# Masked attention on one core: column sums of the exponentials taken by ScalarE's accumulator

## The chip, the cores and the metric

The kernel runs on one core of one Trainium2 chip. The metric is the device time of one execution, in microseconds (us). Before the change, three runs took 752.6, 754.56 and 755.21 us; the median is 754.56.

## What is computed

A residual masked self-attention of 8 batches, 512 features, 1024 tokens, 8 heads of 64 features; queries, keys and values are the same projection. `cond_2048` is the 0/1 mask `mask` of shape (8, 1024).

```python
xt = jnp.transpose(x, (0, 2, 1))
q = xt @ Wq.T
qh = q.reshape(B, T, NH, dk).transpose(0, 2, 1, 3)
scores = scale * jnp.einsum('bhqd,bhkd->bhqk', qh, qh)
logits = (scores * cmask + (1.0 - cmask) * NEG) * rmask
attn = jax.nn.softmax(logits, axis=-1)
ctx = jnp.einsum('bhqk,bhkd->bhqd', attn, qh)
out = ctx.transpose(0, 2, 1, 3).reshape(B, T, D) @ Wo.T
return x + jnp.transpose(out, (0, 2, 1))
```

A kept token attends to the kept tokens. A masked token's logits are all zero, so it gets the mean over all tokens.

## The kernel before

About half the tokens of a batch are kept. The kernel counts them, and where every batch has fewer than 544 it works on 544 columns (`NK`): the kept tokens, packed by an indirect DMA, columns that belong to no token, and as the last column the mean of x, for the masked tokens. Two halves of `KH` = 272 columns make a row of queries. Scores are symmetric, so the sum over the queries in a key's row of the transposed score block is that token's softmax denominator.

The 512 features are four **pairs** of heads, so the program runs over 32 pairs: four per batch, called pair 0 to pair 3 below (`pr` in the code). For each pair there are five **slots** (`k` = 0 to 4): first the short last key block (`LAST`, 32 keys and their copies, tile `el`), then the four key blocks of 128 (tiles `e`). The order of all engines is written out by hand in `late`: each slot issues the scores and exponentials of its block and then whatever the tables and `slots_of` put there.

- `scores` (L605, L609): score matmuls into PSUM tiles `s` (a ring of two tiles of two banks), then exponentials on ScalarE into `e`. Its bias is the tile `bias`.
- `add_up` (L626): sums over the valid queries on VectorE, as a product with a 0/1 row `valid` and an accumulator, one per head and block.
- `invert` with `inverses` (L704 to L709), in slot 0 of the next pair: the sums' inverses, which go to DRAM and come back as rows `rb`; `contexts` in slot 4 multiplies with them.
- `attend_short`, `attend_half` (L642): the products `av` of a pair, in slots 0, 1 and 2 of the next pair.
- `project` (L529) in slot 3 makes `qT` of the pair after next; `values` (L551, L554) in slot 4 transposes it to `v`. `lengths_of` (L563, L565, L572) in slot 1 squares `v` and reduces to `top`; `bias_of` (L578 on TensorE, L580 to L583 on VectorE) in slot 3 (slot 4 in one pair) turns `top` and makes the next pair's `bias`.

Work on other batches lies between. In pairs 0 and 1, `turn` (L417) transposes the next batch's x on VectorE in slots 2 and 4 of pair 0 and 0 and 1 of pair 1, into a ring of two tiles `xt`, and SP stores each to DRAM (`xd`, L425). `search` (L473) finds in pair 1 which token goes to which column, and `gather` (L485) on GpSimd fetches them. `add_features` (L436) sums features on ScalarE with an accumulator in pairs 0 and 1. `output` (L760) multiplies the previous batch's contexts in slots 3 and 4 of pair 1. `finish_blocks` (L829, L832), two operations a step, adds the residual on VectorE from slot 4 of pair 2 to slot 1 of pair 0, eight steps; after the last one SP stores the batch (L839).

SP's DMA queue is in order. Stores wait in the list `stores`, which `issue_stores` empties at the end of a slot, a batch's store one slot later than it was made:

```python
def issue_stores():
    for store in stores[1]:
        store()
    stores[1] = stores[0]
    stores[0] = []
```

Of the kernel before, what the change touches and what calls it, by code (L numbers as in the profile page):

```python
# [305 lines left out]
def attention_of_kept_tokens(ctx, tc, x, mask, wq, wo, out, ident, wqT, woT, verdict, flag):  # L306
# [34 lines left out]
    count = keep.tile([P, LONG], F32, name="count")  # L341
    quadrant = keep.tile([P, A], F32, name="quadrant")
# [10 lines left out]
    sums = [keep.tile([P, 2, NC], F32, name=f"sums_{i}") for i in range(2)]  # L353
# [10 lines left out]
    xs, xbars, xmeans, xds, xins, xcs, valids, searches = {}, {}, {}, {}, {}, {}, {}, {}  # L364
# [13 lines left out]
    def queries_of(b):  # L378

        valid = sb.tile([P, NK], F32, tag="valid", name=f"valid_{b}")  # L380
        nc.gpsimd.tensor_scalar(valid, count[:, :NK], kept[:, b : b + 1], None, ALU.is_lt)  # L381
        part = sb.tile([P, KH], F32, tag="part", name=f"part_{b}")
        for r in range(2):
            rows = slice(r * DK, (r + 1) * DK)
            nc.gpsimd.tensor_copy(part[rows, :], valid[rows, r * KH : (r + 1) * KH])
        valids[b] = valid, part

    def turn_first(i):
# [5 lines left out]
        if i == 0:  # L394
            xds[0] = dr.tile([T, D], F32, tag="xd_0", name="xd_0", bufs=1)
# [13 lines left out]
    def turn(b, i):  # L409
# [4 lines left out]
        if i == 0:  # L414
            xds[b] = dr.tile([T, D], F32, tag="xd", name=f"xd_{b}")
# [50 lines left out]
    def search(b, i):  # L466
# [10 lines left out]
            source[:, col], found[:, col], float(i * P), float(T - 1), ALU.add, ALU.min  # L477
# [42 lines left out]
    def project(pair, hf):  # L520
        b, pr = pair
        nm = f"{b}_{pr}"
        if hf == 0:
            qTs[pair] = sb.tile([P, W], F32, tag="qT", name=f"qT_{nm}", bufs=4)
# [11 lines left out]
        nc.scalar.copy(qT[:, cols], pq[:, :KH])  # L536
# [49 lines left out]
    es, rbs, cTs = {}, {}, {}  # L586

    def scores(pair, c):
        qT, nm = qTs[pair], "%d_%d_%d" % (*pair, c)
        heads = [slice(h * DK, (h + 1) * DK) for h in range(2)]  # L590
        keys = slice(c * P, c * P + (P if c < LAST else DK))
        if c < LAST:
# [4 lines left out]
        for hf in range(2):  # L597
            queries = slice(hf * KH, (hf + 1) * KH)
            to = slice(0, P)
            if c < LAST:  # L600
                s = ps.tile([P, 2, NB], F32, tag="s", name=f"s_{nm}_{hf}")
            else:
                to = slice(hf * DK, (hf + 1) * DK)
            for h in range(2):
                nc.tensor.matmul(  # L605
                    s[to, h, :KH], qT[heads[h], keys], qT[heads[h], queries], start=True, stop=True
                )
            if c < LAST or hf == 1:
                nc.scalar.activation(  # L609
                    e[:, hf if c < LAST else 0, :, :],  # L610
                    s[:, :, :KH],
                    AF.Exp,
                    bias=biases[pair][:, c : c + 1],
                    scale=SCALE,
                )
# [687 lines left out]
```

## Time and profile before

| | |
|---|---|
| median of three runs | 754.56 us (752.6 to 755.21) |
| the profiled execution | 753.0 us, of which the span on the core is 751.3 |
| busy, TensorE matmuls | 658.5 us |
| busy, VectorE | 532.7 us |
| busy, ScalarE | 375.8 us |
| busy, GpSimd | 173.2 us |
| mean granted TensorE clock | 0.925 |

The span is what the profile shows from the first to the last instruction. Busy time is the time in which at least one instruction of the engine ran; matmuls overlap, so their mean durations don't add up to it. PE is TensorE, PEld its weight loads, DVE VectorE, ACT ScalarE, POOL GpSimd, SP and SPq the queue that issues most DMAs. The granted clock is 1.00 at 2.4 GHz and 0.50 at 1.2 GHz. In a row of a timeline, brackets give how long the engine stood idle before it and whose result ended that.

### The profile page before, as it was taken

To read this page: it belongs to the slowest core of one execution; us is meant where nothing else is said; L and a number is where in the kernel's file an instruction comes from. 1 tells how busy PE (TensorE), PEld (TensorE's weight loads), DVE (VectorE), ACT (ScalarE), POOL (GpSimd) and SP (SyncE) were. 2 spreads that over 40 slices of the span, in tenths; PEclk is the share of its full clock that TensorE was granted. 3 is DMA by queue.
4 is the path that set the end of the run, shared out by engine and by line. 5 is a ranking of instruction groups with operands and counts; after the bars stand their busy time and mean duration, and the time that the engine had idled before them with its cause. 6 is when DMAs were issued, how large, how long until landed. Compare 5 with 4: busy or idle time off the path is not lost.

```text
span 751.3 us, 12016 instructions
## 1 busy us (share of the span) xinstructions
PE 658.5 (88%) x4139; PEld 399.7 (53%) x4139; DVE 532.7 (71%) x1560; ACT 375.8 (50%) x771; POOL 173.2 (23%) x222
## 2 busy tenths in 40 slices
PE   5789996999789998799789997799977998999962
PEld 4656664565454655456455664456544565655432
DVE  6179979449992698738996399835999269736761
ACT  5477675266443664256662564526643465425300
POOL 4712010350113410143102511035011440015030
PEclk9799998999889998899988998899988999999985
DMA  7544145845586347934488454774468530654247
GB/s 283 174 138 132 50 149 132 208 135 176 130 196 184 113 159 186 206 126 130 163 201 211 132 158 142 195 186 143 163 154 192 165 114 18 175 139 135 57 137 212
DMA packets 96703, 116.41 MB, mean 155 GB/s; under 512 B 10304, under 2 KB 74304, under 8 KB 96624
## 3 DMA queue, kind: packets, MB, share of 16 engines
q1 hardware_dynamic: 79552, 74.07, 37.4%
q0 software_dynamic: 12848, 39.30, 15.9%
q10 hardware_dynamic: 4224, 2.10, 1.0%
q8 instruction: 36, 0.59, 0.3%
q14 instruction: 43, 0.35, 0.2%
HBM read 72.78 MB, written 42.65 MB: 154 GB/s over the span
## 4 chain that ended last, share of the span: by engine, by line
PE 49%; DVE 37%; DMA 5%; issue 5%; ACT 2%; SPq 1%; POOL 1%; DVEq 0%; POOLq 0%
PE po L760 14%; DVE junk L626 10%; PE pq L529 10%; PE s L605 8%; PE av L642 7%; DVE xt L417 4%; DVE junk L473 4%; DVE o L829 3%; DVE xr L832 3%; PE xc L498 3%; DVE len L565 2%; DVE cT L744 2%; DMA xd<-xt 2%; PE pa L780 2%; DVE rb L739 2%
## 5 line engine op out<-in xcount | busy, mean ns | idle before, releaser
L626 DVE CUSTOM_DVE_ANT_0 junk<-e,valid 128x544 f32<-128x544 f32 x256 | 184.7, 721 | 54.1 <-ACT e L609 47.0
L609 ACT ACTIVATE e<-s,bias 128x544 f32<-128x544 f32 x256 | 168.9, 711 | 29.4 <-PE s L605 25.2
L605 PE MATMUL s<-qT 64*128 64x272 f32 (+1 forms) x1280 | 175.9, 418 | 1.3 <-ACT e L609 1.0
L529 PE MATMUL pq<-xc,wqT 128*128 128x272 f32 x512 | 153.0, 462 | 0.0
L529 PEld LDWEIGHTS pq<-xc,wqT 128*128 128x128 f32 x512 | 117.3, 235 | 28.2 <-issue 0.8
L642 PE MATMUL av<-e,v 128*64 128x272 f32 x1024 | 131.4, 399 | 0.0
L605 PEld LDWEIGHTS s<-qT 64*128 64x128 f32 (+1 forms) x1280 | 92.0, 174 | 71.0 <-issue 30.7
L760 PE MATMUL po<-woT,cT 128*128 128x512 f32 (+1 forms) x448 | 105.5, 434 | 0.0
L536 ACT COPY qT<-pq 128x272 f32<-128x272 f32 x64 | 24.6, 385 | 152.4 <-PE pq L529 152.4
L642 PEld LDWEIGHTS av<-e,v 128*64 128x64 f32 x1024 | 67.9, 136 | 56.0 <-issue 23.1
L485 POOL DMA_INDIRECT xin<-xd,source x40 | 41.5, 1038 | 212.4 <-DVE sums L626 88.0
L760 PEld LDWEIGHTS po<-woT,cT 128*128 128x128 f32 (+1 forms) x448 | 47.7, 150 | 52.7 <-issue 50.7
L861 POOL DMA_INDIRECT g<-od,block_origin x56 | 58.4, 1043 | 33.6 <-issue 17.1
L578 PE MATMUL top<-ident,top 128*128 128x128 f32 x32 | 12.1, 379 | 58.0 <-DVE top L572 57.8
L626 DVE CUSTOM_DVE_ANT_0 junk<-el,part 128x272 f32<-128x272 f32 x64 | 28.3, 442 | 45.9 <-ACT el L609 43.8
L769 POOL DMA_DIRECT2D od<-oc x56 | 30.1, 541 | 130.7 <-ACT oc L767 126.9
L767 ACT COPY oc<-po 128x512 f32<-128x512 f32 (+1 forms) x35 | 18.3, 522 | 81.8 <-PE po L760 81.8
L381 POOL TENSOR_SCALAR valid<-count,kept 128x544 f32<-128x544 f32 x8 | 13.1, 1642 | 138.6 <-DVE sums L704 138.5
L565 DVE TENSOR_REDUCE len<-sq 128x10 f32<-128x640 f32 x32 | 26.0, 813 | 25.7 <-ACT sq L563 25.6
L665 ACT COPY cT<-av 128x272 f32<-128x272 f32 x62 | 23.9, 385 | 39.1 <-PE av L642 39.1
L578 PEld LDWEIGHTS top<-ident,top 128*128 128x128 f32 x32 | 4.8, 151 | 70.9 <-DVE top L572 66.8
L473 DVE TENSOR_SCALAR_CACHE_REDUCE junk<-rank,key 128x1024 f32<-128x1024 f32 (+4 forms) x40 | 39.8, 996 | 1.9 <-ACT rank L1039 1.4
(139 smaller groups left out, 700.7 us busy)
## 6 DMA issues: line engine op xcount, KB each, us to landing
x<-in_x_dram SPq DMA_DIRECT2D x56, 256.0 KB
xd<-xt SPq DMA_DIRECT2D x112, 128.0 KB
xr<-in_x_dram SPq DMA_DIRECT2D x28, 512.0 KB
out_dram<-xr SPq DMA_DIRECT2D x24, 512.0 KB
rb<-row SPq DMA_DIRECT2D x60, 160.0 KB
od<-oc POOLq DMA_DIRECT2D x28, 256.0 KB, 2.5
rank<-ranks SPq DMA_DIRECT2D x6, 512.0 KB
xd<-xt POOLq DMA_DIRECT2D x8, 256.0 KB, 4.5
```

The source lines that it names most:

```text
L417: nc.vector.transpose(xt.rearrange("p k (d f) -> p k d f", d=ND), xs[b][r][:, :, at : at + n].rearrange("p d (k t) -> p k d t", t=Q),)
L473: nc.vector.tensor_scalar(junk[:, :n], rank[:, i * P :], key[:, col], 0.0, ALU.is_le, ALU.add, accum_out=found[:, col])
L485: nc.gpsimd.indirect_dma_start(out=xin[:n, :], out_offset=None, in_=xds[b], in_offset=bass.IndirectOffsetOnAxis(ap=searches[b][2][:n, i : ...
L529: nc.tensor.matmul(pq[:, :KH], wqT[:, d, pr * P : (pr + 1) * P], xcs[b][:, d, cols], start=(d == 0), stop=(d == ND - 1),)
L565: nc.vector.tensor_reduce(lengths, sq.rearrange("p c (h d) -> p (c h) d", h=2), axis=AX.X, op=ALU.add,)
L605: nc.tensor.matmul(s[to, h, :KH], qT[heads[h], keys], qT[heads[h], queries], start=True, stop=True)
L609: nc.scalar.activation(e[:, hf if c < LAST else 0, :, :], s[:, :, :KH], AF.Exp, bias=biases[pair][:, c : c + 1], scale=SCALE,)
L626: nc.vector.tensor_tensor_reduce(junk[:, :n].rearrange("p (f k) -> p f k", k=KH), e[:, :, h, :], (valid if c < LAST else part).rearrange(" ...
L642: nc.tensor.matmul(av[head, :KH], v[keys, c, head], e[keys, hf if c < LAST else 0, h, :], start=(c == first), stop=(c == last),)
L760: nc.tensor.matmul(po[k * n : (k + 1) * n, :w], cTs[b, pr][:, i * P : i * P + n], woT[:, pr, k * w : (k + 1) * w], start=(pr == 0), stop=( ...
L769: nc.gpsimd.dma_start(ods[b][places[i], k * w : (k + 1) * w], oc[k * n : (k + 1) * n, :w])
L861: nc.gpsimd.indirect_dma_start(out=g, out_offset=None, in_=ods[b], in_offset=bass.IndirectOffsetOnAxis(ap=block_origin[:, b, i : i + 1], a ...
```

## The change

The sums over the queries move from VectorE to ScalarE, whose accumulator adds up what an exponential writes. An exponential now covers one head and both halves of the queries, where it covered both heads and one half; so a block's two PSUM tiles hold one head each. The accumulator can't skip columns: those that belong to no token are made zero (the gather takes them from a row of zeros at the end of `xd`, and the mean's column of `qT` stays zero, its value is kept in the copies at the row's end). Each such column adds exp(bias) to a sum; `share` is that exponential, `lacks` the negative count of those columns, and `inverses` takes the product away. The short block `el` is still summed on VectorE (`add_ends`). The values' copy out of PSUM moves from slot 4 to slot 0 of the next pair, behind `el`.

```diff
+    rings = [keep.tile([P, W], F32, name=f"qT_{i}") for i in range(4)]
+    lacks = keep.tile([P, B], F32, name="lacks")
...
-            xds[b] = dr.tile([T, D], F32, tag="xd", name=f"xd_{b}")
+            xds[b] = dr.tile([T + 1, D], F32, tag="xd", name=f"xd_{b}")
+            nc.sync.dma_start(xds[b][T : T + 1, :], zero)
...
-            source[:, col], found[:, col], float(i * P), float(T - 1), ALU.add, ALU.min
+            source[:, col], found[:, col], float(i * P), float(T), ALU.add, ALU.min
...
-        nc.scalar.copy(qT[:, cols], pq[:, :KH])
+        n = KH - hf
+        nc.scalar.copy(qT[:, hf * KH : hf * KH + n], pq[:, :n])
...
     def scores(pair, c):
...
         if c < LAST:
             e = sb.tile([P, 2, 2, KH], F32, tag="e", name=f"e_{nm}", bufs=6)
+            ss = [ps.tile([P, 2, NB], F32, tag="s", name=f"s_{nm}_{h}") for h in range(2)]
+            for hf in range(2):
+                for h in range(2):
+                    nc.tensor.matmul(
+                        ss[h][:, hf, :KH],
+                        qT[heads[h], keys],
+                        qT[heads[h], queries[hf]],
+                        start=True,
+                        stop=True,
+                    )
+            for h in range(2):
+                nc.scalar.activation(
+                    e[:, :, h, :],
+                    ss[h][:, :, :KH],
+                    AF.Exp,
+                    bias=bias,
+                    scale=SCALE,
+                    accum_out=sums[pair[1] % 2][:, h, c : c + 1],
+                )
...
+            share = sb.tile([P, LAST], F32, tag="share", name=f"share_{nm}")
+            nc.scalar.activation(share, biases[pair][:, :LAST], AF.Exp)
...
-    def add_up(pair, c):
+    def add_ends(pair):
 
         b, pr = pair
-        valid, part = valids[b]
-        e = es[pair, c]
+        e = es[pair, LAST]
         for h in range(2):
...
             nc.vector.tensor_tensor_reduce(
-                junk[:, :n].rearrange("p (f k) -> p f k", k=KH),
-                e[:, :, h, :],
-                (valid if c < LAST else part).rearrange("p (f k) -> p f k", k=KH),
-                1.0,
-                0.0,
-                ALU.mult,
-                ALU.add,
-                sums[pr % 2][:, h, c : c + 1],
+                junk[:, :KH], e[:, 0, h, :], parts[b], 1.0, 0.0, ALU.mult, ALU.add, ends[pr % 2][:, h : h + 1]
             )
...
-        for h in range(2):
-            nc.vector.tensor_tensor(acc[:, h, :], acc[:, h, :], pads[:, b, :], ALU.add)
-        nc.vector.tensor_tensor(low, low, acc[:, :, :LAST], ALU.min)
-        nc.vector.tensor_scalar(acc[:, :, :LAST], acc[:, :, :LAST], TINY, None, ALU.max)
+        full = shares.pop(pair)
+        nc.vector.scalar_tensor_tensor(
+            full, full, lacks[:, b : b + 1], pads[:, b, :LAST], ALU.mult, ALU.add
+        )
+        nc.vector.tensor_tensor(acc, acc, full.unsqueeze(1).to_broadcast([P, 2, LAST]), ALU.add)
+        nc.vector.tensor_tensor(low, low, acc, ALU.min)
+        nc.vector.tensor_scalar(acc, acc, TINY, None, ALU.max)
...
-            todo[4].append(lambda: values(ahead))
+            todo[4].append(lambda: turn_values(ahead))
...
-                if k:
-                    add_up(pair, order[k - 1])
+                if k == 0 and p + 1 < len(pairs) and pairs[p + 1] in turned:
+                    copy_values(pairs[p + 1])
+                if k == 1:
+                    add_ends(pair)
                 if k == 0 and before:
-                    add_up(before, order[-1])
```

How the instructions lie afterwards, at three places. First VectorE, from the end of a batch's pair 3 into pair 0 of the next batch (`o` and `xr` are a finish step, `rt` the turned inverses). Before:

```order
L745 COPY cT_2_3491<-qT_2_2940 128x1
L829 STREAM_TRANSPOSE o_5_3612<-g_5_3484 128x512
L832 TENSOR_TENSOR xr_3092<-o_5_3612,xr_3092 128x16x32
L626 ISA junk_3_3_0_3632,sums_87<-e_3_3_3593,valid_2038 128x544
L626 ISA junk_3_3_1_3634,sums_87<-e_3_3_3593,valid_2038 128x544
L704 TENSOR_TENSOR sums_87<-sums_87,pads 128x5 x2
L705 TENSOR_TENSOR low<-low,sums_87 128x8
L706 TENSOR_SCALAR sums_87<-sums_87 128x2x4
L708 RECIPROCAL ris_89<-sums_87 128x2x4
L709 COPY ris_89<-sums_87 128x2
L718 STREAM_TRANSPOSE rt_3_3642<-ris_89 128x32
L829 STREAM_TRANSPOSE o_6_3652<-g_6_3509 128x512
```

The same place with the change:

```order
L772 COPY cT_2_1757<-qT_93 128x1
L856 STREAM_TRANSPOSE o_5_1865<-g_5_1750 128x512
L859 TENSOR_TENSOR xr_1384<-o_5_1865,xr_1384 128x16x32
L728 SCALAR_TENSOR_TENSOR share_3_4_1715<-share_3_4_1715,lacks,pads 128x4
L731 TENSOR_TENSOR sums_88<-sums_88,share_3_4_1715 128x8
L732 TENSOR_TENSOR low<-low,sums_88 128x8
L733 TENSOR_SCALAR sums_88<-sums_88 128x8
L735 RECIPROCAL ris_97<-sums_88 128x2x4
L736 TENSOR_SCALAR ris_97<-ends_90,pads 128x2
L745 STREAM_TRANSPOSE rt_3_1893<-ris_97 128x32
L856 STREAM_TRANSPOSE o_6_1903<-g_6_1775 128x512
```

The two sums over `e` are gone, and the inverses follow the finish step directly; all other places with a 128x544 sum lose it in the same way.

Second ScalarE, at the change from pair 0 to pair 1. Before:

```order
L609 ACTIVATE e_0_3_2134<-s_0_3_0_2135,bias_0_1930 128x544
L609 ACTIVATE e_0_3_2134<-s_0_3_1_2139,bias_0_1930 128x544
L554 COPY v_2_2155<-v_2_0_2156 128x512
L554 COPY v_2_2155<-v_2_4_2162 128x128
L609 ACTIVATE el_1_4_2169<-s_1_4_2170,bias_1_2110 128x544
L609 ACTIVATE e_1_0_2215<-s_1_0_0_2216,bias_1_2110 128x544
```

With the change:

```order
L628 ACTIVATE e_0_3_2015,sums_87<-s_0_3_0_2016,bias_0_1832 128x2x272
L628 ACTIVATE e_0_3_2015,sums_87<-s_0_3_1_2017,bias_0_1832 128x2x272
L645 ACTIVATE el_1_4_2043<-s_1_4_2044,bias_1_1996 128x544
L647 ACTIVATE share_1_4_2050<-bias_1_1996 128x4
L571 COPY v_2_2052<-v_2_0_2032 128x512
L571 COPY v_2_2052<-v_2_4_2037 128x128
L628 ACTIVATE e_1_0_2090,sums_88<-s_1_0_0_2091,bias_1_1996 128x2x272
```

The exponentials write `sums` too, `share` is new, and the copies of `v` stand behind `el`.

Third TensorE, the score matmuls at the same change of pairs. Before:

```order
L605 MATMUL s_1_4_2170<-qT_1_1939 64x272 x4
L642 MATMUL av_0_0_2204<-el_0_4_1985,v_0_1793 64x272 x2
L642 MATMUL av_0_1_2205<-el_0_4_1985,v_0_1793 64x272 x2
L605 MATMUL s_1_0_0_2216<-qT_1_1939 128x272 x2
L605 MATMUL s_1_0_1_2220<-qT_1_1939 128x272 x2
```

With the change:

```order
L642 MATMUL s_1_4_2044<-qT_92 64x272 x4
L666 MATMUL av_0_0_2079<-el_0_4_1875,v_0_1717 64x272 x2
L666 MATMUL av_0_1_2080<-el_0_4_1875,v_0_1717 64x272 x2
L620 MATMUL s_1_0_0_2091<-qT_92 128x272
L620 MATMUL s_1_0_1_2092<-qT_92 128x272
L620 MATMUL s_1_0_0_2091<-qT_92 128x272
L620 MATMUL s_1_0_1_2092<-qT_92 128x272
```

The matmuls are the same four, but they go to the two tiles by turns, where they filled one and then the other.

## Rows read from the trace of the kernel before

**Rows 1.** The page's first section: busy us, share of the span, instructions.

```profile
PE 658.5 (88%) x4139; PEld 399.7 (53%) x4139; DVE 532.7 (71%) x1560; ACT 375.8 (50%) x771; POOL 173.2 (23%) x222
```

**Rows 2.** TensorE's waits: us in total, times, longest us.

```profile
PE top L578 <- DVE top L572: 57.8, 21, 5.7
```

**Rows 3.** Windows: us, busy PE, PEld, DVE, ACT, POOL; clock, DMA share, GB/s.

```profile
101.56:115.76 14.20, 14.20 (x110) 8.85 (x102) 13.43 (x43) 11.20 (x26) 2.56 (x3) 1.00 0.24 63
169.61:184.29 14.68, 14.25 (x110) 8.84 (x102) 14.13 (x39) 8.83 (x18) 0.00 (x0) 1.00 0.47 159
184.29:206.04 21.75, 17.06 (x110) 10.72 (x102) 20.71 (x56) 11.33 (x26) 2.45 (x3) 0.84 0.54 146
241.36:258.12 16.76, 16.76 (x138) 11.03 (x130) 8.99 (x28) 11.20 (x23) 10.49 (x12) 1.00 0.43 136
```

**Rows 4.** Timeline of TensorE: start us, us, what [idle before, releaser].

```profile
47.19 0.32 PE L578 MATMUL top<-ident,top 128*128 128x128 f32 x1 [1.56 <-DVE top L572]
...
129.15 0.48 PE L578 MATMUL top<-ident,top 128*128 128x128 f32 x1 [5.67 <-DVE top L572]
...
196.72 0.47 PE L578 MATMUL top<-ident,top 128*128 128x128 f32 x1 [4.69 <-DVE top L572]
...
205.25 0.69 PE L605 MATMUL s<-qT 64*64 64x272 f32 x8
...
206.33 1.24 PE L605 MATMUL s<-qT 64*128 64x272 f32 x8
...
217.39 0.47 PE L578 MATMUL top<-ident,top 128*128 128x128 f32 x1 [3.62 <-DVE top L572]
...
639.48 0.47 PE L578 MATMUL top<-ident,top 128*128 128x128 f32 x1 [3.80 <-DVE top L572]
```

**Rows 5.** Windows as in rows 3, around two long waits and in batch 0.

```profile
195.60:202.40 6.80, 5.68 (x13) 4.33 (x14) 6.45 (x18) 0.39 (x1) 0.00 (x0) 0.50 0.88 225
639.30:646.10 6.80, 6.62 (x25) 4.83 (x25) 6.34 (x21) 1.25 (x4) 0.00 (x0) 0.75 0.95 234
36.00:52.00 16.00, 12.71 (x74) 8.18 (x73) 12.23 (x33) 10.49 (x26) 3.95 (x5) 1.00 0.47 164
```

**Rows 6.** VectorE by line and form: count, busy us, mean ns, idle before.

```profile
L626 DVE CUSTOM_DVE_ANT_0 junk<-e,valid 128x544 f32<-128x544 f32 x256 | 184.7, 721 | 54.1 <-ACT e L609 47.0
L626 DVE CUSTOM_DVE_ANT_0 junk<-el,part 128x272 f32<-128x272 f32 x64 | 28.3, 442 | 45.9 <-ACT el L609 43.8 <-POOL valid L381 1.0
L565 DVE TENSOR_REDUCE len<-sq 128x10 f32<-128x640 f32 x32 | 26.0, 813 | 25.7 <-ACT sq L563 25.6
```

**Rows 7.** Timeline of VectorE, from pair 0 into pair 1 of batch 2.

```profile
195.04 0.69 DVE L832 TENSOR_TENSOR xr<-o,xr 128x512 f32<-128x512 f32 x1
...
207.52 0.28 DVE L704 TENSOR_TENSOR sums<-sums,pads 128x5 f32<-128x5 f32 x2
...
208.51 0.21 DVE L718 STREAM_TRANSPOSE rt<-ris 128x32 f32<-128x32 f32 x1
209.47 1.25 DVE L417 STREAM_TRANSPOSE xt<-x 128x1024 f32<-128x1024 f32 x1 [0.75 <-DMA xd<-xt]
...
217.17 0.16 DVE L572 TENSOR_REDUCE top<-len 128x1 f32<-128x10 f32 x1
```

**Rows 8.** SP's DMA queue in pair 0 of batch 2.

```profile
195.76 5.08 SPq L839 DMA_DIRECT2D out_dram<-xr  x4
```

**Rows 9.** Timeline of ScalarE: accumulating activations in pair 0, exponentials at a pair's change.

```profile
110.59 0.20 ACT L436 ACTIVATION_READ_ACCUMULATOR junka<-x 128x1 f32 x1
110.82 0.63 ACT L436 ACTIVATE junka<-x 128x512 f32<-128x512 f32 x1
...
204.21 1.32 ACT L609 ACTIVATE e<-s,bias 128x544 f32<-128x544 f32 x2
205.42 0.75 ACT L554 COPY v<-v 128x512 f32<-128x512 f32 x2
...
207.10 1.32 ACT L609 ACTIVATE e<-s,bias 128x544 f32<-128x544 f32 x2 [0.32 <-PE s L605]
```

More of the change, by code (lines that the diff above doesn't have):

```diff
@@ L341, in attention_of_kept_tokens @@
     count = keep.tile([P, LONG], F32, name="count")
+    zero = keep.tile([1, D], F32, name="zero")
     quadrant = keep.tile([P, A], F32, name="quadrant")
@@ L352, in attention_of_kept_tokens @@
     lowest = keep.tile([P, DK], F32, name="lowest")
-    sums = [keep.tile([P, 2, NC], F32, name=f"sums_{i}") for i in range(2)]
+    sums = [keep.tile([P, 2, LAST], F32, name=f"sums_{i}") for i in range(2)]
+    ends = [keep.tile([P, 2], F32, name=f"ends_{i}") for i in range(2)]
+    rings = [keep.tile([P, W], F32, name=f"qT_{i}") for i in range(4)]
+    lacks = keep.tile([P, B], F32, name="lacks")
     ris = [keep.tile([P, Q], F32, name=f"ris_{i}") for i in range(2)]
@@ L394, in turn_first @@
         if i == 0:
-            xds[0] = dr.tile([T, D], F32, tag="xd_0", name="xd_0", bufs=1)
+            xds[0] = dr.tile([T + 1, D], F32, tag="xd_0", name="xd_0", bufs=1)
+            nc.gpsimd.dma_start(xds[0][T : T + 1, :], zero)
         tag = "oc" if i < NC else "xin"
@@ L523, in project @@
         if hf == 0:
-            qTs[pair] = sb.tile([P, W], F32, tag="qT", name=f"qT_{nm}", bufs=4)
+            qTs[pair] = rings[pr % 4]
         qT = qTs[pair]
@@ L541, in project, with turn_values @@
             )
-    def values(pair):
+    turned = {}
+    def turn_values(pair):
         nm = "%d_%d" % pair
         qT = qTs[pair]
-        v = sb.tile([P, NC, P], F32, tag="v", name=f"v_{nm}", bufs=4)
+        turned[pair] = []
         for at, n in ((0, LAST), (LAST, 1)):
@@ L553, in values, with copy_values @@
                 )
+            turned[pair].append((at, n, pt))
+    def copy_values(pair):
+        v = sb.tile([P, NC, P], F32, tag="v", name="v_%d_%d" % pair, bufs=4)
+        for at, n, pt in turned.pop(pair):
             nc.scalar.copy(
@@ L557, in values @@
         vs[pair] = v
+    def values(pair):
+        turn_values(pair)
+        copy_values(pair)
     def lengths_of(pair):
@@ L591, in scores @@
         keys = slice(c * P, c * P + (P if c < LAST else DK))
+        queries = [slice(hf * KH, (hf + 1) * KH) for hf in range(2)]
+        bias = biases[pair][:, c : c + 1]
         if c < LAST:
             e = sb.tile([P, 2, 2, KH], F32, tag="e", name=f"e_{nm}", bufs=6)
+            ss = [ps.tile([P, 2, NB], F32, tag="s", name=f"s_{nm}_{h}") for h in range(2)]
[17 more added lines that the diff above has]
+                )
         else:
@@ L596, in scores @@
             s = ps.tile([P, 2, NB], F32, tag="s", name=f"s_{nm}")
[L597 to L602, printed above, removed]
-                to = slice(hf * DK, (hf + 1) * DK)
-            for h in range(2):
[L605 to L615, printed above, removed]
+            for hf in range(2):
+                to = slice(hf * DK, (hf + 1) * DK)
+                for h in range(2):
+                    nc.tensor.matmul(
+                        s[to, h, :KH], qT[heads[h], keys], qT[heads[h], queries[hf]], start=True, stop=True
+                    )
+            nc.scalar.activation(e[:, 0, :, :], s[:, :, :KH], AF.Exp, bias=bias, scale=SCALE)
+            share = sb.tile([P, LAST], F32, tag="share", name=f"share_{nm}")
+            nc.scalar.activation(share, biases[pair][:, :LAST], AF.Exp)
+            shares[pair] = share
         es[pair, c] = e
-    def add_up(pair, c):
+    def add_ends(pair):
         b, pr = pair
-        valid, part = valids[b]
-        e = es[pair, c]
+        e = es[pair, LAST]
         for h in range(2):
-            junk = sb.tile([P, T], F32, tag="junk", name=f"junk_{b}_{pr}_{c}_{h}", bufs=1)
-            n = NK if c < LAST else KH
+            junk = sb.tile([P, T], F32, tag="junk", name=f"junk_{b}_{pr}_{h}", bufs=1)
             nc.vector.tensor_tensor_reduce(
-                junk[:, :n].rearrange("p (f k) -> p f k", k=KH),
-                e[:, :, h, :],
-                (valid if c < LAST else part).rearrange("p (f k) -> p f k", k=KH),
-                1.0,
-                0.0,
-                ALU.mult,
-                ALU.add,
-                sums[pr % 2][:, h, c : c + 1],
+                junk[:, :KH], e[:, 0, h, :], parts[b], 1.0, 0.0, ALU.mult, ALU.add, ends[pr % 2][:, h : h + 1]
             )
@@ L966, in early @@
         make_identity(nc, ident)
+        nc.gpsimd.memset(zero, 0.0)
         ones = keep.tile([P, P], F32, name="ones")
@@ L1086, in late @@
         queries_of(0)
+        for qT in rings:
+            nc.gpsimd.memset(qT[:, NK - 1 : NK], 0.0)
         load_batch(1, nc.gpsimd)
@@ L1183, in late @@
         last = pairs[-1]
-        add_up(last, order[-1])
         attend_last(last)
```

27 lines of the change are left out of this document (15 added, 12 removed).

## The prediction

> **What bounds the kernel now.** I read the page's first section, then TensorE's waits, then one batch cut at its pairs, then the timelines around the longest waits. TensorE is busy 88% of the span and VectorE 71% [rows 1], so no share says that VectorE matters. TensorE's waits do: 57.8 us of its idle time ends with one operation of VectorE, the maximum `top` from which the next pair's bias is made [rows 2]. Cutting a batch at its `el` exponentials shows where [rows 3]. The windows are, in order, pair 0 of batch 1 (14.2 us, TensorE never idle), then pair 3 of batch 1, pair 0 of batch 2 and pair 2 of batch 2 (pair 1 lies between). Pair 3 takes 14.7 us, with VectorE busy 14.1 of them: it enters pair 0 behind. Pair 0 then takes 21.75 us for the same matmuls that took 14.2 in batch 1. The timeline shows TensorE standing for 4.69 us at `top` in pair 0 of batch 2; it does so in batches 2 to 7, from 4.66 to 4.69 us, the last 3.80. It stands again in pair 1, 5.67 us in batch 1 and 3.62 to 4.04 us in batches 2 to 6 [rows 4]. Pair 0 sums to 27.2 us, pair 1 to 24.9; six waits in pair 3 and a few in batch 0 are the other 5.7.
>
> Each long wait costs twice. After it the granted clock is 0.50, the 1.2 GHz level, and TensorE, back at 196.72, works at half speed until 202.4: 2.85 us lost. The last one is low for half of its 6.8 us window, about 1.6 us lost. Waits up to 1.56 us in batch 0 left the clock at 1.00 [rows 4, 5].
>
> **What leaves VectorE.** 256 sums of 128x544 at 721 ns, 184.7 us [rows 6], 5.8 us of each of 32 pairs; the 64 sums of `el` stay. VectorE no longer carries pair 3's lag into pair 0. From pair 0's `el` matmuls on, it then has the inverses (207.52 to 208.72, 1.2 us), two finish steps of two 0.69 us operations each (1.4 us each), two sums of 0.44 and the reduction `len` at 0.81 with `top` at 0.16 [rows 6, 7]: 5.9 us. Starting 0.9 us after those matmuls, when the last `e` is done, `top` is there at about 6.8. TensorE asks for it at 217.39 - 3.62 - 205.25 = 8.5 us [rows 4]. So pair 0's wait goes, with 1.7 us in hand: 27.2 us, and the clock's 5 x 2.85 + 1.6 = 15.9 us. Pair 3's waits (57.8 - 27.2 - 24.9, less 2.8 in batch 0, or 2.9 us) go too.
>
> **Pair 1 keeps its wait, for another reason.** In batches 2 to 6, VectorE's turn of x in slot 0 of pair 1 waits for a DMA (0.75 us idle, start at 209.47), the store of the turn two before it, whose buffer it takes; from there to `top` it is 217.33 - 209.47 = 7.9 us, with none of the removed sums in it [rows 7]. That store lies in SP's queue behind the 2 MB store of the finished batch, issued at 195.76, right after the last finish step ended at 195.73 [rows 7, 8]: 13.7 us from that issue to the turn. Now the last finish step ends about 6 us into pair 0, so the turn can start at 19.7; pair 0 lasts 14.2 and the 0.55 worked out below, so this is 5.0 us after pair 1's `el` matmuls, against 209.47 - 205.25 = 4.2 before. `top` is 0.8 later and TensorE asks 0.3 to 0.55 later: 0.5 us worse in five batches, **+2.5**, the clock's loss unchanged. In batch 1 no finished batch is stored: the turn follows the inverses at 0.9 + 1.3 = 2.2, `top` comes at 10.1, and 5.67 us become 1.6. By rows 5 such a wait leaves the clock alone: -4.1 and -2.8, **-6.9**.
>
> **What ScalarE gains.** The trace has accumulating activations: the read of the accumulator takes 0.20 us, and the next accumulating activation starts 0.23 us after the read's start [rows 9]. Two exponentials run 1.21 us apart from their successor, 0.605 each, so an accumulating one holds ScalarE 0.83 us: 0.23 more, 1.84 a pair, and about 0.2 for the tiny exponential `share`, an estimate after the read's 0.20. In pair 0 ScalarE was busy 11.2 of 14.2 us [rows 3]; 13.3 still fits. The Trainium skill (ScalarE: Activation LUTs, Rules for kernel authors) says that `add` belongs on VectorE and not on ScalarE; by that rule the 256 reads of 0.20 us would count in full, and the sum would be 753 + 51 = 804. The rows speak against it: VectorE is the late engine, and ScalarE has room.
>
> **What the PSUM tiles cost.** A block's four score matmuls filled one tile and then the other, so the first exponential began 0.77 us after them (206.33 to 207.10) [rows 4, 9]. Now each tile takes matmuls 1 and 3 or 2 and 4, and the first exponential waits for the second half too: 0.56 us later. Where two blocks and `el` follow closely, at a change of pairs, this reaches TensorE: block 3's exponentials start at 204.77 for 204.21, the second 0.83 later, `el` at 206.43 and it ends, at an exponential's 0.71, at 207.15. The next pair's first block needs `el`'s tile at its second matmul, about 206.6: 0.55 us of wait, where the view of waits shows next to none today. Elsewhere 2 us of `av` matmuls lie between blocks. It strikes at the starts of pairs 0, 1 and 3, not of pair 2, ahead of which the output matmuls stand; and pair 1 waits anyway. Two per batch and a few in batch 0, 18 in all: **+10** (bounds 0, if the exponentials catch up, and 1.1 each, +20, if a tile is also held through the read of 0.20 and ScalarE's copies push in).
>
> The values' copy moves behind `el`; it frees its banks for the `av` matmuls that come four banks later, so nothing waits for it. On VectorE the inverses have six operations before and after. The zero rows are eight 2 KB stores on queues that idle there. The mask's GpSimd work shrinks, off the path. All nothing.
>
> **Sum**, against the profiled execution's 753.0 us (0.2% under the median of 754.56): 753.0 - 27.2 - 15.9 - 2.9 + 2.5 - 6.9 + 10 = 712.6, **713 us**.
>
> **Rivals.**
> *Pair 1's wait goes too* (12%): if the store's landing does not hold the turn, since only 0.75 us of idleness is put down to it. Then 5 x (3.84 + 0.5 + 2.85) = 36 us more go: 677. Against it: the turn starts only when 2.5 MB have left in 13.7 us, with DMA 0.88 to 0.95 busy [rows 5].
> *The tie through PSUM is stronger* (20%): 1.1 us at 18 starts and some 0.15 us in the blocks of the eight pairs 0, where ScalarE is fullest: 728.
> *The wait is not the sums'* (4%): the finish steps and the bias chain alone hold `top`, pair 0 keeps most of its wait, about 753. The 5.8 us a pair against a wait of 4.7 speak against it.
> *ScalarE becomes the bound* (2%, slower): an accumulating exponential that costs x more makes pair 0 11.4 + 8x, pair 3 9.0 + 8x, pair 2 11.4 + 8x, against 14.7, 14.7 and 16.8 of TensorE. At x = 0.83 eight batches lose 8 x (3.3 + 0.9 + 1.2) = 43 us, and the gain is gone; at 1.0, some 788. The rows show 0.23.
> *The clock falls at each change of pairs* (4%, slower): TensorE's new 0.55 us waits each bring the 1.2 GHz level and 2.85 us of loss: 18 x 2.85 = 51, so 764; it decides from 0.8 of them. Rows 5 speak against it, with waits of 0.7 to 1.56 us at 1.00. The Trainium skill (TensorE: Matmul & The Clock Gate, A second HAM failure mode: psum-queue depth-cycling) tells of a kernel whose short TensorE idles, from cycling through PSUM, made the clock swing; by that rule the trace should show it in batch 0, and it doesn't.
>
> **The numbers.** 58% for my forecast, whose own range is 700 to 724 (the PSUM term from 0 to 20). A measurement here tells 0.3% from no change. Faster are the forecast, the first two rivals: 90%; same is the third, 4%; slower the last two, 6%. The range goes from 676 to 732: it takes in both faster rivals and the bounds, and leaves out the rest and the tails.
>
> **What would show it.** Right: no `junk` of 128x544 with `e` on VectorE; 256 reads of 0.2 us on ScalarE; `top` waits of TensorE down from 57.8 to about 26 us, nearly all in pair 1 of batches 2 to 6; pair 0 at 14.7 us and granted 1.00; low-clock stretches between batches 1 and 7 from twelve to five; new TensorE waits for `el` of half a microsecond. Wrong: pair 0 still standing over 3 us (the third rival), pair 1 without a wait (the first), TensorE waiting for `e` within pairs (the second or fourth), or clock 0.50 where no wait over 1.6 us went before.

## The result

The changed kernel takes 723.75 us (median of four runs, 722.87 to 726.28) where the kernel before, run beside it, takes 754.88 (752.6 to 755.35). The ratio is 0.960, with a 95% interval of 0.957 to 0.963: faster. The profiled execution takes 723.6 us with a span of 721.9: 29.4 us under the one before, where the forecast's sum had 40.4. Of the kernels in the experiments below, two have one execution of four that lies more than 1.5% above their fastest (723.33 us with the store in halves, 705.28 with the products shared out evenly); without it their medians are 713.64 and 692.80.

The page of the changed kernel (section 1, then the chain of work followed back from the last instruction, by engine, then groups of section 5):

```profile
PE 656.5 (91%) x4139; PEld 400.6 (55%) x4139; DVE 353.6 (49%) x1049; ACT 401.2 (56%) x1059; POOL 163.8 (23%) x220
...
PE 75%; DVE 12%; DMA 4%; SPq 3%; issue 2%; ACT 2%; POOL 0%; DVEq 0%
...
L628 ACT ACTIVATE e<-s,bias 128x544 f32<-128x544 f32 x256 | 180.4, 709 | 62.8 <-PE s L620 59.1
L620 PE MATMUL s<-qT 64*128 64x272 f32 x1024 | 169.4, 418 | 1.8 <-ACT e L628 1.6
...
L628 ACT ACTIVATION_READ_ACCUMULATOR e<-s,bias 128x1 f32 x256 | 50.2, 196 | 0.0
```

VectorE went from 532.7 us to 353.6 [rows 1], 179.1 less for the 184.7 of its sums [rows 6]. ScalarE's busy time grew by 25.4 us, though 256 reads of 0.196 us are 50.2: about half of a read overlaps its neighbours. TensorE's matmuls on `s` are busy 169.4 us; the same matmuls took 153.9 before. That growth is waiting which the view counts as busy, as the timelines below show.

TensorE's waits, then one of VectorE's, of the changed kernel (us in total, times, longest):

```profile
PE top L599 <- DVE top L593: 25.2, 7, 5.6
...
PE s L642 <- ACT e L628: 3.9, 20, 0.2
```

```profile
DVE xt L426 <- DMA xd<-xt: 19.4, 5, 4.7
```

The wait for `top` fell from 57.8 us in 21 places [rows 2] to 25.2 in seven: five of 4.3 to 5.6 us in pair 1 of batches 2 to 6, one of 0.85 in pair 1 of batch 1, one of 0.81 in batch 0. New is a wait of 0.2 us for `e` ahead of the `el` scores, twenty times.

Windows of the changed kernel, columns as in [rows 3] and the same four stretches: pair 0 of batch 1, pair 3 of batch 1, pair 0 of batch 2, pair 2 of batch 2.

```profile
106.47:121.37 14.90, 14.71 (x110) 9.14 (x106) 9.07 (x28) 11.98 (x36) 0.00 (x0) 1.00 0.32 77
169.11:183.94 14.83, 14.64 (x108) 9.21 (x102) 11.98 (x33) 9.75 (x26) 1.98 (x2) 1.00 0.61 202
183.94:198.78 14.84, 14.65 (x109) 9.21 (x102) 10.47 (x29) 12.00 (x34) 0.00 (x0) 1.00 0.58 136
235.96:253.41 17.45, 17.26 (x138) 11.44 (x130) 6.09 (x19) 12.14 (x33) 9.71 (x12) 1.00 0.45 144
```

Pair 0 of batch 2 lost 6.9 us and runs at 1.00. Pair 0 of batch 1, which had no wait, got 0.7 us longer, and so did pair 2. Cutting the whole span in this way, from one `el` exponential to the next, gives every class of pairs against the forecast (us, batches 1 to 7 unless named, the profiled executions):

| stretch | forecast | measured |
|---|---|---|
| pair 0, seven | -39.3 | -38.6 |
| pair 1, seven | -4.4 | -3.4 |
| pair 2, seven | 0 | +5.8 |
| pair 3, batches 1 to 6 | +0.4 | +0.6 |
| last pair and tail | +0.6 | +1.3 |
| start and batch 0 | +2.2 | +4.9 |
| sum | -40.5 | -29.4 |

The big terms hold to a microsecond. Of the 11 us that are missing, 5.8 lie in pair 2 and 2.7 in batch 0.

TensorE's timeline of the changed kernel (start us, us, what, idle before): in batch 0, the `top` of pair 1 of batches 1 and 2, a change from pair 2 to pair 3.

```profile
43.00 1.88 PE L620 MATMUL s<-qT 64*128 64x272 f32 x8 [0.19 <-ACT e L628]
45.65 2.87 PE L620 MATMUL s<-qT 64*128 64x272 f32 x8 [0.78 <-ACT e L628]
48.63 0.48 PE L599 MATMUL top<-ident,top 128*128 128x128 f32 x1
...
130.37 0.32 PE L599 MATMUL top<-ident,top 128*128 128x128 f32 x1 [0.85 <-DVE top L593]
...
212.51 0.47 PE L599 MATMUL top<-ident,top 128*128 128x128 f32 x1 [5.57 <-DVE top L593]
...
252.63 0.69 PE L642 MATMUL s<-qT 64*64 64x272 f32 x8 [0.19 <-ACT e L628]
253.14 0.64 PE L666 MATMUL av<-el,v 64*64 64x272 f32 x8
253.70 1.65 PE L620 MATMUL s<-qT 64*128 64x272 f32 x8
```

ScalarE's at the same change:

```profile
251.77 0.71 ACT L628 ACTIVATE e<-s,bias 128x544 f32<-128x544 f32 x1 [0.59 <-PE s L620]
252.38 0.19 ACT L628 ACTIVATION_READ_ACCUMULATOR e<-s,bias 128x1 f32 x1
252.47 0.70 ACT L628 ACTIVATE e<-s,bias 128x544 f32<-128x544 f32 x1
253.07 0.20 ACT L628 ACTIVATION_READ_ACCUMULATOR e<-s,bias 128x1 f32 x1
253.41 0.71 ACT L645 ACTIVATE el<-s,bias 128x544 f32<-128x544 f32 x1
```

The eight score matmuls of a pair's first block take 1.65 us where they took 1.24 [rows 4]; the wait lies inside the group, so the view of waits doesn't list it. Accumulating exponentials start 0.70 us apart, where those before were 0.605 apart: a read adds 0.09 us, not the 0.23 forecast.

The finished batch's store in SP's queue, in pair 0 of batch 2, and VectorE's turn of x in pair 1 that waits behind it:

```profile
190.34 5.21 SPq L866 DMA_DIRECT2D out_dram<-xr  x4
```

```profile
204.58 1.25 DVE L426 STREAM_TRANSPOSE xt<-x 128x1024 f32<-128x1024 f32 x1 [4.73 <-DMA xd<-xt]
```

Windows over low-clock stretches of the changed kernel, batch 0 first, then two after waits in pair 1:

```profile
46.30:53.10 6.80, 6.69 (x18) 4.59 (x18) 2.91 (x7) 4.49 (x12) 0.00 (x0) 0.50 0.25 52
210.10:216.90 6.80, 4.39 (x11) 3.35 (x12) 6.38 (x20) 0.25 (x1) 0.08 (x1) 0.50 0.91 235
295.50:298.90 3.40, 3.24 (x8) 2.54 (x9) 3.16 (x14) 0.00 (x0) 0.00 (x0) 0.50 0.96 213
```

Between batches 1 and 7 the granted clock is low in five stretches instead of twelve. The one in batch 0 is new: the same place stood at 1.00 before [rows 5].

### The profile page after: what moved, and what is told of

It reads as the page before. It is cut to its first block, busy times and chain, and to the rows that moved or that the text cites. A ratio compares the mean times of both kernels' runs of the same rounds, so it can differ in the third digit from the quotient of the medians.

```text
span 721.9 us, 11836 instructions
## 1 busy us (share of the span) xinstructions
PE 656.5 (91%) x4139; PEld 400.6 (55%) x4139; DVE 353.6 (49%) x1049; ACT 401.2 (56%) x1059; POOL 163.8 (23%) x220
## 4 chain that ended last, share of the span: by engine, by line
PE 75%; DVE 12%; DMA 4%; SPq 3%; issue 2%; ACT 2%; POOL 0%; DVEq 0%
PE s L620 17%; PE av L666 16%; PE pq L538 15%; PE po L787 14%; DVE junk L482 3%; SPq L434 3%; DVE xt L426 3%; PE xc L507 3%; PE s L642 2%; DMA xd<-xt 2%; PE pa L807 2%; PE top L599 1%; DMA g<-od,origin 1%; ACT e L628 1%; PE v L563 1%
## 5 line engine op out<-in xcount | busy, mean ns | idle before, releaser
L628 ACT ACTIVATE e<-s,bias 128x544 f32<-128x544 f32 x256 | 180.4, 709 | 62.8 <-PE s L620 59.1
L620 PE MATMUL s<-qT 64*128 64x272 f32 x1024 | 169.4, 418 | 1.8 <-ACT e L628 1.6
L620 PEld LDWEIGHTS s<-qT 64*128 64x128 f32 x1024 | 98.1, 186 | 68.0 <-ACT e L628 22.5
L538 PE MATMUL pq<-xc,wqT 128*128 128x272 f32 x512 | 134.4, 419 | 0.0
L538 PEld LDWEIGHTS pq<-xc,wqT 128*128 128x128 f32 x512 | 104.2, 209 | 22.0 <-issue 0.8
L494 POOL DMA_INDIRECT xin<-xd,source x40 | 39.3, 984 | 294.4 <-PE pq L538 154.3
L731 DVE TENSOR_TENSOR sums<-sums,share 128x8 f32<-128x8 f32 x32 | 5.4, 167 | 114.7 <-ACT e L628 114.5
L796 POOL DMA_DIRECT2D od<-oc x56 | 30.3, 543 | 121.1 <-ACT oc L794 117.4
L628 ACT ACTIVATION_READ_ACCUMULATOR e<-s,bias 128x1 f32 x256 | 50.2, 196 | 0.0
L601 DVE TENSOR_REDUCE m<-top 128x1 f32<-128x128 f32 x32 | 9.3, 290 | 77.0 <-PE top L599 77.0
L426 DVE STREAM_TRANSPOSE xt<-x 128x1024 f32<-128x1024 f32 x28 | 34.7, 1241 | 19.8 <-DMA xd<-xt 19.4
L859 DVE TENSOR_TENSOR xr<-o,xr 128x512 f32<-128x512 f32 x56 | 38.8, 692 | 1.9
```

The lines of the kernel that those rows point to most:

```text
L426: nc.vector.transpose(xt.rearrange("p k (d f) -> p k d f", d=ND), xs[b][r][:, :, at : at + n].rearrange("p d (k t) -> p k d t", t=Q),)
L494: nc.gpsimd.indirect_dma_start(out=xin[:n, :], out_offset=None, in_=xds[b], in_offset=bass.IndirectOffsetOnAxis(ap=searches[b][2][:n, i : ...
L538: nc.tensor.matmul(pq[:, :KH], wqT[:, d, pr * P : (pr + 1) * P], xcs[b][:, d, cols], start=(d == 0), stop=(d == ND - 1),)
L620: nc.tensor.matmul(ss[h][:, hf, :KH], qT[heads[h], keys], qT[heads[h], queries[hf]], start=True, stop=True,)
L628: nc.scalar.activation(e[:, :, h, :], ss[h][:, :, :KH], AF.Exp, bias=bias, scale=SCALE, accum_out=sums[pair[1] % 2][:, h, c : c + 1],)
L796: nc.gpsimd.dma_start(ods[b][places[i], k * w : (k + 1) * w], oc[k * n : (k + 1) * n, :w])
```

## The experiments

Three things are to be told apart. First, whether the gain is VectorE's sums, or something else that came with the change (the new tiles, the copy of `v`). Second, what holds pair 1: the finished batch's store ahead of the turned x in SP's queue, or VectorE's own work. Third, what costs pairs 0, 2 and 3 and batch 0 their microseconds: the scores that fill two PSUM tiles by turns, or the accumulator's reads. Where an expectation names a theory by a letter, A is the account held when that run was planned, which is not always the prediction's, and later letters are its rivals. The four runs of the first group shared one chip, on which the kernel before took 763.61 us; the second group's took 761.25, the third's 755.05. So times are compared within a group, and ratios are to the kernel before on the same chip. The changed kernel itself ran beside the second group only.

**The store after the turns.** The finished batch's store goes behind the last store of turned x:

```diff
-            stores[0].append(store)
+            (held if b + 2 < B else stores[0]).append(store)
...
-        for store in stores[1]:
+        for store in stores[1] + (held if last_turn else []):
...
-                issue_stores()
+                issue_stores((pr, k) == (1, 1))
```

> The finished batch's store is issued after the turns' stores of pair 1 instead of before those of pair 0. Theory A (the wait that is left in pair 1 comes from the 2 MB store standing ahead of the turned x in SP's queue): TensorE's waits for top in pair 1 of batches 2 to 6 fall from 4.3 to 5.6 us to 1.6 us or less, no 1.2 GHz stretch follows them, and the time falls from 724 to about 697. Rival B (VectorE's own chain in pair 1, turns and searches, is what holds top): waits and time stay, 721 to 727.

Measured: 729.98 us, ratio 0.955 (0.951 to 0.959), little under the changed kernel's 0.960 on its own chip. Waits of TensorE, and one of VectorE, in this kernel:

```profile
PE s L642 <- ACT e L628: 11.9, 18, 4.2
PE s L620 <- ACT el L645: 9.4, 4, 4.8
...
PE top L599 <- DVE top L593: 6.3, 8, 0.9
```

```profile
DVE rb L763 <- DMA rb<-row: 13.9, 5, 5.0
```

The `top` waits of pair 1 are gone, and pair 1 takes 30.3 us in all of batches 1 to 6 (changed kernel: 35.2 to 37.2 in batches 2 to 6). So that store did hold it. But part of the gain comes back in the next two pairs: SP's DMA queue of this kernel (start us, us, what) in pairs 1 to 3 shows the store, then the next load, then the rows `row` and `rb` of the inverses:

```profile
213.06 5.49 SPq L866 DMA_DIRECT2D out_dram<-xr  x4
226.72 2.00 SPq L851 DMA_DIRECT2D xr<-in_x_dram  x4
228.76 3.38 SPq L748 DMA_DIRECT2D row<-rt  x4
243.13 1.09 SPq L753 DMA_DIRECT2D rb<-row  x2
```

`rb` follows `row` after 14.4 us; a pair earlier, with no store ahead of it, it follows in 2.3 (204.31 and 206.65). VectorE stands at `rb` in five places, for up to 5.0 us. Pair 2 of batches 2 to 6 takes 21.6 us on average, 2.6 more than in batch 1 of the same run, and pair 3 16.7, 1.9 more. Not all of that is the store's: in the third run of this group, which has the store in its old place and no accumulators, the same pairs take 19.9 and 15.3 us. Against that run some 3 us of the 6 gained in pair 1 are given back, and five low-clock stretches remain between batches 1 and 7. The 2 MB delay what is issued behind them in either place.

**The sums on VectorE as well**, into a tile that nothing reads:

```diff
+                elif k:
+                    add_again(pair, order[k - 1])
                 if k == 0 and before:
+                    add_again(before, order[-1])
```

> VectorE does its 256 sums of 128x544 again, into a tile that nobody reads; ScalarE's accumulators stay. Theory A (the gain is VectorE's freed time in pairs 3 and 0): pair 0's wait of about 4.7 us comes back with its low clock, 724 + 43 = 767, above the kernel before, because the tie through PSUM stays. Rival B (the gain is the new order: copies behind el, inverses that wait for ScalarE alone): 724 to 730.

Measured: 791.94 us, ratio 1.036 (1.031 to 1.041), 54 us over the next kernel below, on the same chip, which has neither these sums nor the accumulators. The expected 767 was missed by 25 us; this chip accounts for some 9 of them (763.61 us for 754.88 with the kernel before), and the rest was not looked into. TensorE's wait for `top` is back in the view of waits:

```profile
PE top L600 <- DVE top L594: 62.0, 17, 6.9
```

Pair 0 of batches 2 to 7 takes 18.2 to 20.6 us instead of 14.8. Everything else of the change is there, so the gain is the sums leaving VectorE. That this kernel is slower than the one before fits that: it pays for the tie through the PSUM tiles and gets nothing for it.

**No accumulator, and then also a tile per half again.** The first run takes the accumulator off; the second gives each PSUM tile one half of the queries for both heads, as before the change. Both leave the sums of the four long blocks out; `sums` is set to 1 once, at the start.

```diff
-                    accum_out=sums[pair[1] % 2][:, h, c : c + 1],
```

```diff
-                        ss[h][:, hf, :KH],
+                        ss[hf][:, h, :KH],
...
-                    e[:, :, h, :],
+                    e[:, h, :, :],
...
-                    accum_out=sums[pair[1] % 2][:, h, c : c + 1],
```

> The exponentials keep one head each and their PSUM tiles, but write no accumulator (the sums are left out and taken as 1). Theory A (an accumulator's read holds ScalarE 0.09 us, and only two of them at a pair's change reach TensorE): 718 to 723. Rival B (ScalarE is the bound): 256 x 0.09 to 0.20 us go, 700 or less.

> As the run without accumulators, and the PSUM tiles hold one half of the queries with both heads again, as before the change (sums left out and taken as 1). Theory A (each tile filled by turns delays a block's first exponential by 0.45 us, and TensorE loses about 0.6 us at nearly all 31 changes of pairs): 18 us less than 724, about 705. Rival B (my term as predicted, 0.55 us at 18 of them): about 714 less what the reads give. Rival C (the loss is not there): as the run without accumulators.

Measured: 737.51 us (0.964, 0.959 to 0.968) and 724.63 us (0.949, 0.944 to 0.953). Undisturbed pairs 0 and 3 take 14.84 to 14.89 us with the accumulator, 14.75 to 14.80 without it, and 14.12 to 14.18 with tiles per half. So eight reads cost 0.09 us a pair, and filling two tiles by turns costs 0.6. (Five such pairs of the two runs took 0.3 to 2.5 us more and are left out.) In the time of the whole kernel the reads don't show: 0.964 without them, 0.960 with them on another chip; the tiles are worth 12.9 us on one chip, for 18 expected. TensorE's timeline at a change to pair 0 in the last one:

```profile
178.72 0.76 PE L563 MATMUL v<-ident,qT 128*128 128x128 f32 x5
179.42 0.69 PE L641 MATMUL s<-qT 64*64 64x272 f32 x8
...
180.49 1.19 PE L620 MATMUL s<-qT 64*128 64x272 f32 x8
```

No idle time ahead of `el`, and 1.19 us for the first block. From one row's start to the next, in the changed kernel: 0.96 us instead of 0.70 from the transposes of `v` to the `el` scores, and 1.55 to 1.61 instead of 1.12 for the first block. That is 0.26 and 0.43 to 0.49 us, 0.7 together. Whether another order alone would do, both matmuls of one head and then both of the other, was not run. Batch 0 shows the same: its pair 0 takes 17.87 us in the first run, and 15.11 in the second, which has no low clock there. Not all of it reaches the end: with 0.6 us off pairs 0 and 3, pair 1 waits longer (36.4 to 39.3 us; `top` 32.5 us in all, for 23.5).

**The store in halves, the products earlier, and both.** The store of the finished batch is issued after four finish steps and after eight, 1 MB each; then half 0's `av` matmuls move from slot 1 to slot 0, ahead of the first scores, and half 1's to slots 1 and 2. A run of the changed kernel stands beside them.

```diff
-        n = NT if b + 2 < B else G
+        n = G
```

```diff
-            for hf in range(2):
-                todo[1 + hf].append(lambda hf=hf: attend_half(before, hf))
+            todo[0].append(lambda: attend_half(before, 0))
+            todo[1].append(lambda: attend_half(before, 1, (0, 1)))
+            todo[2].append(lambda: attend_half(before, 1, (2, 3)))
```

> The changed kernel itself, beside the next three on the same chip: 0.96 of the kernel before.

> The finished batch's store is cut in two: its first half goes after four of the eight finish steps, in pair 3, where the DMA engines idle; only the second half is ahead of the turned x in SP's queue. Theory A (the queue holds pair 1's top): the waits of TensorE in pair 1 of batches 2 to 6 fall under 2 us, the low clock after them goes, and with no later transfer pushed back the time falls by up to 27 us against the changed kernel, 3.7%. Rival B (VectorE's own chain holds it): no change. Rival C (the wait goes, but the DMA engines are the bound and it comes back later, as with the store put off): 1% or less.

> The av matmuls of the pair before are moved: the first half stands in slot 0, ahead of the first block's scores, the second half is split over slots 1 and 2. Theory A (the first block's scores wait 0.4 us for el's tile at each of 31 changes of pairs): that wait is covered by 2 us of av matmuls, 12 us less than the changed kernel, 1.7%, with 0.2 us at el's own scores left. Rival B (my predicted 18 places): 7 us. Rival C (ScalarE is late by itself, the wait moves to the next block): no change.

> Both edits. Theory A: the two gains add up, as one is in pair 1 and the other at the changes of pairs: up to 39 us less than the changed kernel, about 0.91 of the kernel before. Rival: the larger of the two alone.

Measured: the changed kernel 740.72 us (0.975, 0.969 to 0.982), the store in halves 713.66 (0.942, 0.934 to 0.949), the products earlier 742.93 (0.978, 0.973 to 0.983), both 718.38 (0.942, 0.939 to 0.946). On this chip the change is worth less: its pairs 2 of batches 1 to 6 take 19.1 to 20.6 us for 17.45. The runs of the first group have such pairs 2 too (18.6 to 20.9 us without the accumulators). Why stays open.

The store in halves gives 27 us. Pair 1 of batches 2 to 6 falls from 36.1 us on average to 31.0, which is 25 of them, and TensorE's wait for `top` is nearly gone:

```profile
PE top L599 <- DVE top L593: 9.8, 7, 3.1
```

Unlike the store put last, this takes nothing back: pair 3 stays at 14.83 to 14.89 us, pair 2 takes 18.7 to 19.6, on average less than in the changed kernel beside it (19.1 for 19.7), and between batches 1 and 7 no stretch has the low clock. The expectation calls the DMA engines idle in pair 3, where the first half now goes; in the changed kernel they were busy for 0.61 of it (169.11 to 183.94).

The products earlier give nothing. TensorE's timeline at a pair's start there:

```profile
260.25 2.05 PE L666 MATMUL av<-e,v 128*64 128x272 f32 x16
262.23 1.19 PE L620 MATMUL s<-qT 64*128 64x272 f32 x8
263.35 1.14 PE L666 MATMUL av<-e,v 128*64 128x272 f32 x8
264.42 1.77 PE L620 MATMUL s<-qT 64*128 64x272 f32 x8
```

The first block runs at 1.19 us, but the next, with half as many products ahead of it, takes 1.77. The wait moved by one block, and pairs 0 and 3 got longer (15.57 and 15.28 us for 14.85). In these rows a block of scores runs at 1.19 us with 2 us of products ahead of it, and not with 1.1. With the store in halves the products earlier give nothing either.

**Products shared out evenly, and batch 0's feature sums later.** With the store in halves: alone again; with two blocks' products ahead of the first scores, three ahead of the second and three ahead of the third; and then also with the eight `add_features` of batch 0 moved from pairs 0 and 1 into pairs 1 and 2, and `mean_of`, which needs them, behind them.

```diff
+            todo[0].append(lambda: attend_half(before, 0, (0, 1)))
+            todo[1].append(lambda: attend_half(before, 0, (2, 3)))
+            todo[1].append(lambda: attend_half(before, 1, (0,)))
+            todo[2].append(lambda: attend_half(before, 1, (1, 2, 3)))
```

```diff
+        FEATURES_LATER = {(1, 1): (0,), (1, 2): (1,), (1, 3): (2, 3), (2, 0): (4, 5), (2, 1): (6, 7)}
...
-                    for i in FEATURES.get((pr, k), ()):
+                    for i in (FEATURES if b else FEATURES_LATER).get((pr, k), ()):
```

> The kernel with the store cut in two, once more, beside the next two on the same chip: 0.94 of the kernel before.

> The store cut in two, and the av matmuls of the pair before laid evenly between the score blocks: two blocks' worth in slot 0, three in slot 1, three in slot 2 (1.5 us each, where slot 0 had none of them, and where the moved ones of the earlier run left 1 us in two slots). Theory A (a block's scores stand only where less than about 1.2 us of other matmuls lie ahead of them): the 0.42 us at the first block of 31 pairs go and nothing takes their place, 13 us less than the run beside it; pairs 0 and 3 at 14.4 us instead of 14.84. Rival B (ScalarE's chain through a pair is what holds TensorE, the wait turns up at another block): no change or some us slower.

> The same, and in batch 0 the eight sums of features on ScalarE move from pairs 0 and 1 to pairs 1 and 2. Theory A (pair 0 of batch 0 is long because ScalarE is full there, TensorE's short waits add up and the clock falls): it goes from 18.4 us to about 15, no 1.2 GHz stretch around 46 us, 3 us less. Rival B (it is the start of the pipeline that makes that pair long): no change.

Measured: 698.06 us (0.925, 0.923 to 0.928), 696.92 (0.923, 0.916 to 0.930), 696.19 (0.920, 0.917 to 0.924). All three are far under the kernel before; the changed kernel did not run on this chip, and its 0.960 is from another. Among themselves the intervals overlap. In the first of them VectorE's waits for the turned x are down to

```profile
DVE xt L426 <- DMA xd<-xt: 1.9, 5, 0.9
```

and pair 1 takes 30.4 to 31.2 us. Where the even sharing's expected gain went, TensorE's timeline of the second shows, at the start of a pair 0:

```profile
182.20 0.69 PE L642 MATMUL s<-qT 64*64 64x272 f32 x8 [0.19 <-ACT e L628]
...
184.35 1.19 PE L620 MATMUL s<-qT 64*128 64x272 f32 x8
185.46 1.60 PE L666 MATMUL av<-e,v 128*64 128x272 f32 x12
186.99 1.31 PE L620 MATMUL s<-qT 64*128 64x272 f32 x8
188.23 1.60 PE L666 MATMUL av<-e,v 128*64 128x272 f32 x12
189.75 1.46 PE L620 MATMUL s<-qT 64*128 64x272 f32 x8
```

The first block's 0.44 us are gone, the 0.19 ahead of `el` stays, and the two blocks behind take 0.12 and 0.27 longer. Pair 0 comes out at 14.94 us for 14.87, pair 3 at 14.67 for 14.86, pair 2 at 17.15 for 17.45: 0.4 us a batch, some 3 us in all (the spans of the two profiled executions are 690.0 and 693.0), which these runs can't tell from nothing.

The feature sums do what they were moved for. In batch 0 the third kernel's waits are 0.46 and 0.50 us, its pair 0 takes 15.26 us instead of 17.88, and the clock over the place that was low in the changed kernel is 1.00:

```profile
46.00:53.00 7.00, 6.31 (x36) 4.42 (x38) 2.65 (x7) 3.38 (x10) 0.00 (x0) 1.00 0.32 76
```

In its profiled execution two pairs 1 took 35.3 and 33.1 us and gave that back; 2.98 us of one are a wait for `top`. So its own worth is shown in batch 0, and not in the median.

## Why the prediction held, and where it missed

The forecast was 713 us with a range of 676 to 732, and 700 to 724 for its own case; 723.75 lies at the edge of that case. Its steps, in order:

- *What leaves VectorE*: right. Pair 0 of batches 2 to 6 lost 6.91 us each, forecast 6.97 with the clock's 2.85 and the tie's 0.55; the last one 4.76 for 4.85. The run with the sums on VectorE as well shows that it is the sums.
- *Pair 1 keeps its wait*: right, and because of the store, as forecast; that the size fits is partly luck. From the store's issue to the turn it was 13.7 us before, and is 14.2 now (190.34 to 204.58), though VectorE is free earlier: its own wait for that DMA grew from 0.75 us [rows 7] to 4.73. Moving or halving the store takes the wait away. In those 14.2 us the DMA engines are busy for 0.91 to 0.98 of the time, so whether the store holds the turn by its place in the queue or by filling the engines is not told apart. The five pairs got 3.0 us longer together, forecast 2.5. But their waits for `top` grew by 4.3 us (23.5 for 19.2), and the tie, which the forecast left out there, lengthens these pairs too; against that, the low clock, taken as unchanged, lasts 3.4 us instead of 6.8 after three of the five waits. Batch 1's pair 1 lost 6.85 us for 6.9, with a wait of 0.85 us for 1.6. The rival that the wait goes too fell on this.
- *What ScalarE gains*: the size was wrong, and harmless. A read adds 0.09 us between exponentials, not 0.23; the 0.23 was taken from accumulating activations of another line, whose one result tile may have spaced them, which was not tried. The rule of the Trainium skill (ScalarE: Activation LUTs, Rules for kernel authors) that `add` belongs on VectorE is stated for the rate per element, and the page's section does not speak of an accumulator. So the forecast's 804 was its own stretch of that rule, and it left VectorE's gain out; measured were 723.6 us, and 0.09 us a pair for all eight reads.
- *What the PSUM tiles cost*: this step failed, in size and place. It was one wait of 0.55 us at 18 changes of pairs; it is two, 0.26 us ahead of `el` and 0.44 inside the first block, and "not of pair 2, ahead of which the output matmuls stand" was wrong: pair 2 got 0.7 us longer in six batches and 1.5 in the last. The output matmuls stand ahead of `el`, but between `el` and the first block there are only 0.6 us of products, as in every pair. The bound of 1.1 us a change was too high, the count of 18 too low: 0.7 us at 31 changes would be some 22 us, an estimate, where the term was 10; the run with a tile per half gave 12.9 back. The runs without the accumulator show the cause: 0.6 us go with the way in which the tiles are filled, and 0.09 with the reads.
- *The clock falls at each change of pairs*: wrong as a rule and right in one place. Waits of 0.19 us at twenty changes left it at 1.00. But in batch 0, after waits of 0.19 and 0.78 us, 6.8 us at 1.2 GHz are new, which the forecast had named as a sign of being wrong; the 16 projection matmuls there take 5.9 us where they took 3.83, and pair 0 of batch 0 3.7 us more in all. The forecast had taken from waits of 0.7 to 1.56 us in batch 0, which left the clock at 1.00 [rows 5], that shorter ones would too. The Trainium skill (TensorE: Matmul & The Clock Gate, A second HAM failure mode: psum-queue depth-cycling) tells of a clock that swings with short idles from cycling through PSUM. Batch 0 is the one place where the trace fits that, with a single fall that is not there with a tile per half; nowhere else does it.

Of the 11 us that are missing, pair 2's 5.8 and pair 0's 0.7 are mostly the tie, and batch 0's 2.7 the clock with the tie; pair 1's 1.0, the tail's 0.7 and pair 3's 0.2 are the rest.

## What to carry to other kernels

An engine that is busy 71% of the span can still be the late one: cut a batch at its pairs, see which engine's work ends last in each, and take work off that engine, to one that has room there. When accumulators ask for another split of the PSUM tiles, look at when the first evacuation can start; matmuls that fill two tiles by turns delay it and show up as longer matmuls, not as waits. A large store delays what is issued behind it in the same queue wherever it stands, so try cutting it up (27 us here) before moving it (some 6 us a batch saved in one pair, some 3 lost in two others).

## What was not expected

The low clock of batch 0 came where the waits listed are shorter than in the kernel before. Both kernels over the same 4 us, which in the changed one end just ahead of the fall (windows as in [rows 3], the changed kernel first, then the one before), and two rows of TensorE in the one before:

```profile
42.00:46.00 4.00, 3.03 (x17) 1.79 (x15) 1.44 (x2) 3.86 (x11) 0.00 (x0) 1.00 0.45 104
42.00:46.00 4.00, 2.62 (x18) 1.29 (x16) 3.00 (x7) 4.00 (x11) 0.00 (x0) 1.00 0.01 4
```

```profile
42.10 1.19 PE L605 MATMUL s<-qT 64*128 64x272 f32 x8
44.30 1.33 PE L605 MATMUL s<-qT 64*128 64x272 f32 x8 [1.01 <-ACT e L609]
```

The view has TensorE busier ahead of the fall, but the block of scores that took 1.19 us takes 1.88 there, and such a stretched row holds waiting that counts as busy: 17 matmuls ran in these 4 us, and 18 in the kernel before. So this does not show that TensorE stood less. What decides is not settled by these runs; they only show that the fall goes with the tiles filled by turns together with batch 0's feature sums, and that taking away either ends it.

The same kernel differed between chips more than the kernel before did: 723.75 and 740.72 us for the changed one, 754.88 and 761.25 for the one before beside it. Most of the extra time is in pair 2 (19.1 to 20.6 us for 17.45), and its cause was not looked for by a run.
